# Layer-norm statistics of two tokens in one bn_stats instruction

## The chip, the cores and the metric

The kernel runs on one core of a Trainium2 chip. The core has a matrix engine (TensorE, PE in the profile), a vector engine (VectorE, DVE), a scalar engine (ScalarE, ACT), a general engine (GpSimd, POOL) and a queue of DMA commands (SyncE, SP). Each engine works through a list of instructions of its own in a fixed order and waits where an instruction needs what another engine has not finished. The metric is the device time of one execution in microseconds. The profile is one execution taken by the hardware profiler.

## The reference

The input is 32 images of 56 x 56 tokens with 96 channels each. Everything is float32 but for the feed-forward part, which rounds to small float formats.

```python
# layer 0: per token layer norm, matmul, 3 x 3 convolution
mu = jnp.mean(x, axis=-1, keepdims=True)
var = jnp.mean(jnp.square(x - mu), axis=-1, keepdims=True)
h = (x - mu) * jax.lax.rsqrt(var + LN_EPS) * ln_w + ln_b
x1, z = jnp.split(jnp.einsum('bhwc,cd->bhwd', h, w_in) + b_in, 2, axis=-1)
x = x + jax.nn.silu(conv3x3(x1) + conv_b)
# layer 1: attention by a Fourier transform over the 3136 tokens of an image
t = to_tokens(x)
t = t + bn2(w2 @ real(ifft(relu_mix(fft(relu(bn1(w1 @ ln(t)))))))) 
t = t + ffn(ln(t))           # 96 -> 384 -> 96, products of rounded values
```

So each token passes three layer norms. Each needs the mean and the variance of its 96 channels.

## The kernel before

**Layout.** An image lies in SBUF as 112 partitions x 28 tokens x 96 channels, so the channels of a token are next to each other in one partition. It is loaded in four chunks (LN_CHUNKS) of 8, 8, 8 and 4 tokens per partition. Most work goes by groups g of four tokens per partition, seven of them (NG) in an image.

**Three norms.** `stats(t, kind, b, i)` is called once for each kind, image and chunk. Kind "a" is the norm ahead of the convolution (tile xl, called in `take_in`), kind "b" the norm ahead of the Fourier part (tile t, in `conv_part`, as soon as the two groups of a chunk have been added), kind "c" the norm ahead of the feed-forward part (tile t again, in `back`). The tile t has 97 columns per token. The last column is for kind b, where L144 writes the square root of the variance into it.

**What stats does before.** One `bn_stats` for each token (L130) reads 96 channels and writes six numbers: a count, a mean and a sum of squared deviations of the channels in even places, and the same three of the channels in odd places. Five small instructions, each on all tokens of the chunk (8 or 4 columns), join the halves: the difference d of the two means (L135), the sum of the two squared sums with epsilon (L136), the mean for kind c alone (L139), and the variance with the term of d (L140 and L141). GpSimd raises the variance to the power of -1/2 (L142). For kinds a and b no mean is wanted, because the centring is folded into the weights that follow. `norm` runs on GpSimd: L153 subtracts the mean (kind c), L154 multiplies by the factor of L142.

**What runs beside it.** Four images are in flight. The outer loop over k has two parts in every turn. In the first, the spectrum part, TensorE does the second half of the Fourier transform (px at L252, pg at L279, pe at L284) and VectorE the mixing between them, five instructions each time (L266 to L271). In the second part, for each g, `forth` starts the transform of the next image (ph at L224, pa at L229), `back` ends that of the present one (py at L304; L305 adds py to t and frees its PSUM buffer, of which ph and px take the same two in turn) and calls stats c, and `ffn` runs the feed-forward part with a lag of four groups. There TensorE computes pf (L314), ScalarE rounds it to h1 (L316), VectorE adds the bias and clips (h2, L318) and rounds (hq, L319), TensorE multiplies again (po, L326), ScalarE and VectorE round and add (L330, L332), and GpSimd adds the result to t (L333). A list of pieces of later images, `filler`, is spread over both parts: the convolution (cv at L201), its adding to the image (L210), stats b, and stats a with the norm of an image further ahead.

**Order.** The kernel's text gives the instructions, the tile framework's scheduler gives each engine its order and the waits. The statistics tile, d and var come from the pool `stp` with three buffers for each tag, mean and factor from `sums` with eight.

Of the kernel before, what the change touches and what calls it, by code (L numbers as in the profile page):

```python
# [38 lines left out]
F32 = mybir.dt.float32  # L39
# [3 lines left out]
ALU = mybir.AluOpType  # L43
AX = mybir.AxisListType

C = 96
HW = 56
N = HW * HW
N1, N2 = 112, 28
# [12 lines left out]
EPS = 1e-5  # L62
# [17 lines left out]
def hybrid_kernel(ctx: ExitStack, tc: tile.TileContext, x, par, w_in, conv_w, w1, w2, fw1, fb1, fw2, fb2, fa, fb, ib, ia, on, out):  # L80
    nc = tc.nc
# [36 lines left out]
    sums = ctx.enter_context(tc.tile_pool(name="sums", bufs=8))  # L118
    stp = ctx.enter_context(tc.tile_pool(name="stp", bufs=3))
# [3 lines left out]
    def stats(t, kind, b, i):  # L123


        n = t.shape[1]
        name = f"{kind}_{b}_{i}"
        st = stp.tile([N1, n, 2, 3], F32, tag="st6", name=f"st6_{name}")
        for j in range(n):
            nc.vector.bn_stats(st[:, j].rearrange("p h s -> p (h s)"), t[:, j, :C])  # L130
        d = stp.tile([N1, n], F32, tag="d", name=f"d_{name}")
        var = stp.tile([N1, n], F32, tag="var", name=f"var_{name}")
        mu = None
        rs = sums.tile([N1, n], F32, tag=f"rs{kind}", name=f"rs_{name}")
        nc.vector.tensor_tensor(d, st[:, :, 0, 1], st[:, :, 1, 1], ALU.subtract)  # L135
        nc.vector.scalar_tensor_tensor(var, st[:, :, 0, 2], C * EPS, st[:, :, 1, 2], ALU.add, ALU.add)  # L136
        if kind == "c":
            mu = sums.tile([N1, n], F32, tag="mu", name=f"mu_{name}")
            nc.vector.scalar_tensor_tensor(mu, d, 0.5, st[:, :, 1, 1], ALU.mult, ALU.add)  # L139
        nc.vector.scalar_tensor_tensor(d, d, 0.25, d, ALU.mult, ALU.mult)  # L140
        nc.vector.scalar_tensor_tensor(var, var, 1.0 / C, d, ALU.mult, ALU.add)  # L141
        nc.gpsimd.tensor_tensor(rs, var, mhalf[:, :n], ALU.pow)  # L142
        if kind == "b":
            nc.vector.tensor_tensor(t[:, :, C], var, rs, ALU.mult)  # L144
        return mu, rs

    def norm(t, mu_rs, kind, b, i):

# [215 lines left out]
    def take_in(im, i):  # L364

        if i + 1 < len(LN_CHUNKS):
            fetch(im, i + 1)
        xl = im.xl.pop(i)
        im.xa += norm(xl, stats(xl, "a", im.b, i), "a", im.b, i)
# [8 lines left out]
    def conv_part(im, g):  # L378

        if g % 2 == 0 and g < NG:  # L380
            im.load(g // 2)
        if g < NG:
            im.s[g] = conv(im.strips.pop(g), im.b, g)
        if g >= 1:
            conv_add(im.s.pop(g - 1), im.group(g - 1, im.x), im.group(g - 1)[:, :, :C], im.b, g - 1)
            for i in ended(g - 1):
                im.rs[i] = stats(im.t[i], "b", im.b, i)[1]
# [18 lines left out]
    def back(im, g):  # L406

        transform_out(im.y.pop(g), im.group(g)[:, :, :C], im.b, g)
        fetch_y(im, g + 3)
        for i in ended(g):  # L410
            im.xc += norm(im.t[i], stats(im.t[i], "c", im.b, i), "c", im.b, i)
# [71 lines left out]
    with tc.tile_pool(name="setup", bufs=1) as sp, tc.tile_pool(  # L483
        name="setup_ps", bufs=2, space=bass.MemoryType.PSUM
# [247 lines left out]
```

## Time and profile before

| what | value |
|---|---|
| time, median of three runs | 4002.35 us (3998.4 to 4002.89) |
| span of the profiled execution | 3996.6 us |
| TensorE busy | 3660.6 us, 92% |
| VectorE busy | 2669.3 us, 67% |
| ScalarE busy | 2196.9 us, 55% |
| GpSimd busy | 1283.2 us, 32% |
| bn_stats, three kinds | 2,688 instructions, 509.1 us |

The busy time of an engine counts overlapping instructions once, so the sum over groups is larger than the busy time. In a line of a group, the first number behind the bar is the busy time in us, then the mean duration of one in ns; behind the second bar stands how long the engine was idle just before the instructions of the group, and who ended it. In a line of the timeline, start and duration in us come first, and a number in brackets is the idle time ahead of it with what ended it. A line of waits names who waited for whom, the total in us, how many times, and the longest.

### The profile page before, as it was taken

The page shows a single profiled execution, that of the slowest core. Times are in us where ns is not written, and L with a number is a line of the kernel's source. Part 1 is how long each engine was busy: PE and PEld are TensorE (multiplying, and loading weights), DVE is VectorE, ACT ScalarE, POOL GpSimd, SP SyncE. Part 2 cuts the span into 40 slices and gives each one's busy share as a digit, 9 for nine tenths or more (in the row PEclk, how much of TensorE's full clock was granted, in tenths as well). Part 3 has the DMA queues.
Part 4 walks back from the last instruction along what each step waited for, and adds up shares of the span by engine and source line. Part 5 has one row for each costly group of instructions (what it writes and reads, how often), then busy time and mean ns, then how long its engine had stood idle before and what let it go on. Part 6 is the DMA issues. An engine that isn't in the chain of part 4 may idle for free. (4 is left out here: it accounts for less than half of the span.)

```text
span 3996.6 us, 70615 instructions
## 1 busy us (share of the span) xinstructions
PE 3660.6 (92%) x22229; PEld 2482.5 (62%) x22229; DVE 2669.3 (67%) x9014; ACT 2196.9 (55%) x5154; POOL 1283.2 (32%) x1004
## 2 busy tenths in 40 slices
PE   5899999999999999999999999999999999999986
PEld 3566666566666566665566665666665666665665
DVE  3366677676677676677676676766676766676666
ACT  1355555555555555555555555555555555555564
POOL 2133223333233333233332233332243332243322
PEclk9999999999999999999999999999999999999996
DMA  5554455554555554545554445545545555555531
GB/s 137 141 151 133 135 140 139 143 150 137 138 138 140 145 149 137 137 128 149 142 144 130 134 136 140 156 136 139 138 137 141 152 138 136 140 137 143 143 87 52
DMA packets 582492, 546.30 MB, mean 137 GB/s; under 512 B 172584, under 2 KB 535304, under 8 KB 581896
## 3 DMA queue, kind: packets, MB, share of 16 engines
q1 hardware_dynamic: 578402, 539.17, 49.5%
q8 instruction: 180, 2.95, 0.3%
q10 hardware_dynamic: 3720, 2.63, 0.3%
q14 instruction: 190, 1.56, 0.1%
HBM read 346.93 MB, written 194.25 MB: 135 GB/s over the span
## 5 line engine op out<-in xcount | busy, mean ns | idle before, releaser
L201 PE MATMUL cv<-k,wp 128*96 128x448 f32 (+1 forms) x3136 | 1368.8, 550 | 21.6 <-ACT s L203 12.6
L201 PEld LDWEIGHTS cv<-k,wp 128*96 128x96 f32 (+1 forms) x3136 | 462.5, 165 | 385.1 <-issue 334.0
L316 ACT CAST h<-pf 128x448 f16<-128x448 f32 x672 | 358.7, 534 | 433.7 <-PE pf L314 415.3
L305 DVE TENSOR_TENSOR t<-py,t 112x384 f32<-112x384 f32 x224 | 124.5, 556 | 628.4 <-PE py L304 628.4
L153 POOL TENSOR_TENSOR xn_c<-t,mu_c 112x768 f32<-112x768 f32 (+1 forms) x128 | 169.0, 1321 | 1028.1 <-DVE var_a L136 826.4
L252 PE MATMUL px<-fb_sb,at 112*96 112x112 f32 (+1 forms) x3584 | 431.2, 263 | 24.8 <-DVE sv L268 18.9
L252 PEld LDWEIGHTS px<-fb_sb,at 112*96 112x96 f32 x3584 | 383.6, 165 | 78.9 <-DVE sv L268 30.3
L279 PE MATMUL pg<-w2a,gt 96*112 96x96 f32 (+1 forms) x3584 | 416.8, 264 | 12.9 <-DVE gt L271 10.8
L227 ACT ACTIVATE h<-ph,rs_b 112x192 f32<-112x192 f32 x896 | 325.2, 419 | 186.1 <-PE ph L224 175.1
L326 PEld LDWEIGHTS <-hq 128*112 128x112 fp8e5 x2688 | 207.7, 134 | 331.0 <-DVE hq L319 281.8
L224 PE MATMUL ph<-w1a,n2t 97*112 97x192 f32 x1792 | 365.1, 332 | 42.4 <-DVE t L305 41.7
L279 PEld LDWEIGHTS pg<-w2a,gt 96*112 96x112 f32 (+1 forms) x3584 | 383.1, 179 | 27.4 <-PE st L209 12.8
L318 DVE TENSOR_SCALAR h<-h,b1q 128x448 f16<-128x448 f16 x672 | 350.6, 522 | 62.7 <-ACT h L316 59.2
L203 ACT ACTIVATE s<-cv,par_sb 96x448 f32<-96x448 f32 x224 | 141.5, 632 | 456.5 <-PE cv L201 456.5
L142 POOL TENSOR_TENSOR rs_a<-var_a,mhalf 112x8 f32<-112x8 f32 (+1 forms) x128 | 199.4, 1558 | 590.0 <-DVE var_a L141 554.8
L142 POOL TENSOR_TENSOR rs_b<-var_b,mhalf 112x8 f32<-112x8 f32 (+1 forms) x128 | 192.4, 1503 | 587.7 <-DVE var_b L141 413.5
L326 PE MATMUL po<-w2q,hq 128*112 128x96 fp8e5 x2688 | 251.1, 220 | 141.7 <-DVE hq L319 131.6
L229 PE MATMUL pa<-h,fa_sb 112*112 112x384 f32 x896 | 369.4, 508 | 6.0 <-ACT h L227 1.4
L333 POOL TENSOR_TENSOR o<-t,y 112x384 f32<-112x384 f32 x224 | 201.2, 898 | 447.4 <-DVE y L332 261.2
L224 PEld LDWEIGHTS ph<-w1a,n2t 97*112 97x112 f32 x1792 | 281.3, 177 | 94.3 <-DVE t L305 61.3
L319 DVE CAST hq<-h 128x448 fp8e5<-128x448 f16 x672 | 315.6, 470 | 16.1
L266 DVE SCALAR_TENSOR_TENSOR sv<-px,par_sb,av 96x224 f32<-96x224 f32 (+1 forms) x448 | 197.8, 442 | 174.1 <-ACT av L264 172.8
(106 smaller groups left out, 6387.7 us busy)
## 6 DMA issues: line engine op xcount, KB each, us to landing
k<-img SPq DMA_DIRECT2D x2464, 58.0 KB
da<-u SPq DMA_DIRECT2D x224, 336.0 KB
at<-da SPq DMA_DIRECT2D x224, 336.0 KB
img<-stage SPq DMA_DIRECT2D x224, 174.0 KB
de<-es SPq DMA_DIRECT2D x224, 168.0 KB
y<-de SPq DMA_DIRECT2D x224, 168.0 KB
out<-o SPq DMA_DIRECT2D x224, 168.0 KB
xl<-in_x SPq DMA_DIRECT2D x96, 336.0 KB
```

What stands on the lines that cost most here:

```text
L142: nc.gpsimd.tensor_tensor(rs, var, mhalf[:, :n], ALU.pow)
L201: nc.tensor.matmul(ps, wp[: seen.shape[0], k, :], seen, start=(k == 0), stop=(k == 6))
L224: nc.tensor.matmul(ph[:, j, :], n2t[:, 2 * j2 + j, :], w1a, start=True, stop=True)
L227: nc.scalar.activation(h[:, j], ph[:, j], AF.Relu, scale=rs[:, 2 * j2 + j : 2 * j2 + j + 1])
L229: nc.tensor.matmul(pa, fa_sb, h, start=True, stop=True)
L252: nc.tensor.matmul(px[:, j], ats[g][:, j, i * C : (i + 1) * C], fb_sb[:, first(p) : first(p + 1)], start=True, stop=True)
L279: nc.tensor.matmul(pg[:, j, :], lhs, w2a[:, i, :], start=(i == 0), stop=(i == 1))
L316: nc.scalar.copy(h1, pf)
L318: nc.vector.tensor_scalar(h2, h1, b1q[:, k : k + 1], 0.0, ALU.add, ALU.max)
L319: nc.vector.tensor_copy(hq[:, k, :], h2, saturate=False)
L326: nc.tensor.matmul(po[:, j, :], hq[:, k, j * N1 : (j + 1) * N1], w2q[:, k, :], start=(k == 0), stop=(k == 2))
L333: nc.gpsimd.tensor_tensor(o, tg, y2, ALU.add)
```

## The change

One `bn_stats` now takes two tokens. It reads them channel by channel in turn: channel 0 of the first, channel 0 of the second, channel 1 of the first, and so on. The even places are then the first token and the odd places the second, so the six numbers are the statistics of two whole tokens and nothing has to be joined. What is left is one instruction per chunk: the sum of squared deviations divided by 96, plus epsilon. The mean for kind c is read where bn_stats wrote it, with a step of three. The statistics tile has a tag for each kind; d and mu are no longer there. It is for fewer instructions on VectorE.

```diff
-        st = stp.tile([N1, n, 2, 3], F32, tag="st6", name=f"st6_{name}")
-        for j in range(n):
-            nc.vector.bn_stats(st[:, j].rearrange("p h s -> p (h s)"), t[:, j, :C])
-        d = stp.tile([N1, n], F32, tag="d", name=f"d_{name}")
+        st = stp.tile([N1, n, 3], F32, tag=f"st{kind}", name=f"st_{name}")
+        for j in range(0, n, 2):
+            nc.vector.bn_stats(
+                st[:, j : j + 2].rearrange("p j s -> p (j s)"), t[:, j : j + 2, :C].rearrange("p j c -> p c j")
+            )
         var = stp.tile([N1, n], F32, tag="var", name=f"var_{name}")
-        mu = None
+        nc.vector.tensor_scalar(var, st[:, :, 2], 1.0 / C, EPS, ALU.mult, ALU.add)
         rs = sums.tile([N1, n], F32, tag=f"rs{kind}", name=f"rs_{name}")
-        nc.vector.tensor_tensor(d, st[:, :, 0, 1], st[:, :, 1, 1], ALU.subtract)
-        nc.vector.scalar_tensor_tensor(var, st[:, :, 0, 2], C * EPS, st[:, :, 1, 2], ALU.add, ALU.add)
-        if kind == "c":
-            mu = sums.tile([N1, n], F32, tag="mu", name=f"mu_{name}")
-            nc.vector.scalar_tensor_tensor(mu, d, 0.5, st[:, :, 1, 1], ALU.mult, ALU.add)
-        nc.vector.scalar_tensor_tensor(d, d, 0.25, d, ALU.mult, ALU.mult)
-        nc.vector.scalar_tensor_tensor(var, var, 1.0 / C, d, ALU.mult, ALU.add)
         nc.gpsimd.tensor_tensor(rs, var, mhalf[:, :n], ALU.pow)
         if kind == "b":
             nc.vector.tensor_tensor(t[:, :, C], var, rs, ALU.mult)
-        return mu, rs
+        return (st[:, :, 1] if kind == "c" else None), rs
```

The lines of the kernel after the change stand five lower from L142 on (L142 becomes L137).

## The prediction

> **What bounds the kernel now.** I read the page first (busy shares, then the slices), then the waits of TensorE in the steady stretch, then the groups of the lines that the change touches, and last the timeline of one image.
>
> ```profile
> PE 3660.6 (92%) x22229; PEld 2482.5 (62%) x22229; DVE 2669.3 (67%) x9014; ACT 2196.9 (55%) x5154; POOL 1283.2 (32%) x1004
> PE   5899999999999999999999999999999999999986
> DVE  3366677676677676677676676766676766676666
> ```
>
> TensorE (PE) is busy in nine tenths of every slice but the first two and the last two; VectorE (DVE), where the whole change lies, is at two thirds. So VectorE's own busy time is not the time of the kernel. What counts is how often TensorE stands waiting for it. Between 250 and 3780 us TensorE is busy for 3296.59 of 3530 us: it idles 233 us there, and some 103 us more in start and end. The waits of TensorE in that stretch, longest first:
>
> ```profile
> PE po L326 <- DVE hq L319: 119.0, 123, 2.1
> PE ph L224 <- DVE t L305: 41.7, 29, 2.6
> PE px L252 <- DVE sv L268: 18.1, 57, 0.4
> PE pf L314 <- DVE n3t L310: 12.6, 30, 0.4
> PE cv L201 <- ACT s L203: 9.7, 29, 0.3
> PE pg L279 <- DVE gt L271: 8.2, 29, 0.5
> ```
>
> Columns: total us, times, longest. About 200 us of the 233 have VectorE as releaser, none of them a line of the statistics. The statistics matter only as what stands ahead of L319 and L305 in VectorE's queue. The groups that go:
>
> ```profile
> L130 DVE BATCH_NORM_STATS2 st_a<-xl 112x6 f32<-112x96 f32 x896 | 172.4, 245 | 80.3 <-DMA xl<-in_x 80.3
> L141 DVE SCALAR_TENSOR_TENSOR var_c<-var_c,d_c 112x8 f32<-112x8 f32 (+1 forms) x128 | 79.3, 620 | 2.3
> L140 DVE SCALAR_TENSOR_TENSOR d_c<-d_c 112x8 f32<-112x8 f32 (+1 forms) x128 | 52.8, 412 | 0.2
> L136 DVE SCALAR_TENSOR_TENSOR var_c<-st_c 112x8 f32<-112x8 f32 (+1 forms) x128 | 20.5, 160 | 0.0
> ```
>
> One operation of eight columns takes 160 ns, yet L141 averages 620. The timeline of one stall shows why:
>
> ```profile
> 2061.16 0.56 DVE L305 TENSOR_TENSOR t<-py,t 112x384 f32<-112x384 f32 x1 [1.75 <-PE py L304]
> 2061.76 0.74 DVE L130 BATCH_NORM_STATS2 st_c<-t 112x6 f32<-112x96 f32 x4
> 2062.53 0.83 DVE L135 TENSOR_TENSOR d_c<-st_c 112x8 f32<-112x8 f32 x1
> ...
> 2063.89 1.27 DVE L141 SCALAR_TENSOR_TENSOR var_c<-var_c,d_c 112x8 f32<-112x8 f32 x1
> ...
> 2067.03 1.41 DVE L141 SCALAR_TENSOR_TENSOR var_a<-var_a,d_a 112x8 f32<-112x8 f32 x1
> 2068.36 0.54 DVE L305 TENSOR_TENSOR t<-py,t 112x384 f32<-112x384 f32 x1
> ```
>
> ```profile
> 2063.64 1.49 POOL L153 TENSOR_TENSOR xn_c<-t,mu_c 112x768 f32<-112x768 f32 x1 [0.32 <-DVE mu_c L139]
> 2066.95 1.47 POOL L154 TENSOR_TENSOR xn_c<-xn_c,rs_c 112x768 f32<-112x768 f32 x1
> ```
>
> ```profile
> 2068.96 0.90 PE L224 MATMUL ph<-w1a,n2t 97*112 97x192 f32 x4 [2.40 <-DVE t L305]
> ```
>
> The reader sees a queue, not a dependence. Between two L305 lie 12 bn_stats, the small operations and two L141 that end with GpSimd's L153 and L154. L305 comes 7.20 us after its predecessor, and TensorE loses 2.40 us.
>
> [...] 1.27 and 1.41 us for an operation that else takes 0.16, ending with GpSimd's 1.49 and 1.47. [...] L305 and L130 keep their durations here. [...] the timeline has eight bn_stats within 1.36 us, (1.36-0.245)/7 = 159 ns from start to start. [...] The new bn_stats alternates between two tokens. No instruction of the trace reads SBUF so; the nearest, ScalarE's L203, reads PSUM alternately from two halves and takes 632 ns for 448 elements, where the plain copy L215 takes 537, so 1.2 times.
>
> **The change part by part.**
> 1. bn_stats: 2,688 of 96 elements become 1,344 of 192. A pair occupies VectorE for 2 x 159 = 318 ns now. [...] I take the full rate: [...] the L203 comparison points the same way.
> 2. Small operations: L135, L136, L140, L141 go in 384 chunks and L139 in 128, 1,664 in all; 384 tensor_scalar come. The timeline has them 85 ns apart, so -1,280 x 0.085 = -109 us.
> 3. Waiting for GpSimd inside them: over 0.163 us each, L141 of c and a, L140 of c and L135 of c hold 58, 42, 32 and 19 us, 151 us in all. I do not expect all to go: [...] the mean now needs no work, so L153 is released by the last bn_stats itself and can start just ahead of the tensor_scalar. I count half, -75 us; the ends are 0 and -151.
> 4. L153 reads its mean from the statistics tile with a step of three. It has its own three buffers for c, freed when L153 ends, a whole chunk before they are wanted. GpSimd runs the same 1,004 instructions and has two thirds of its time free: nothing.
> 5. Order. A scheduler places the work; in the changed program the TensorE order of a steady image is the same but for a few transposes and matmuls moved by one or two places. On VectorE, in the stretch of the stall above, 8 bn_stats of pairs and two tensor_scalar stand between the L305 of group 3 and that of group 4, and near the end of an image the add of h2 stands ahead of the column write (L144) that waits some 1.8 us for GpSimd's rs, not behind it.
>
> Sum for VectorE: -78 - 109 - 75 = -262 us of 2669. Most of that lies beside a busy TensorE. What reaches the end: (a) the stall on L305. Of its 7.20 us, L305 and L210 keep 1.1; [...] two small ones 0.2, and one or two waits for GpSimd 1.2 to 2.4 make 4.6 to 5.8. That is 1.4 to 2.6 us earlier, against a mean stall of 41.7/29 = 1.44 us; I take off 30 of 41.7 us. (b) L319: 119/29 = 4.1 us per image. The last piece, 1.99 us in the image that I read, is caused by L144 standing ahead of h2, and half of it should go; another, 1.26 us, is an L318 that met L154 of the next image, which now comes 1.5 us earlier and may miss it. The others are GpSimd meetings that the change does not touch. I take 1 us per image, 30 us. (c) Start and end: the chain of the last image holds L141 of c (1.24 us), and the first image passes four such; 3 us. Sum -63 us: 4002 - 63 = 3939, say 3940 us.
>
> **The rivals.** There are three.
> The alternating read is slow [...]. [...] In (a) [...] about 10 us of gain; in (b) the last piece only, 12 us. 4002 - 25 = 3977 us.
>
> TensorE hides nearly everything: the stalls on L319 stay, since GpSimd's L153, L154 and L333 meet L318 and L319 whatever the statistics cost, and L305 gains a little. For: the 119 us are mostly such meetings. Against: 41.7 us stand behind the statistics alone. 3998 us.
>
> Slower: [...] With 1 us per image lost, 4002 + 32 = 4034 us. A moved meeting with GpSimd ahead of L319 would end in the same place.
>
> **How the numbers follow.** Full rate and gains as summed: 0.5. Slow read with a small gain: 0.24. Nothing to be seen: 0.1. Slower: 0.16. The first two are faster by more than 0.2% (8 us), but a part of the second falls short of it, so faster 0.72, same 0.1, slower 0.18. The lower end of the range is the forecast with all of the 151 us gone, the whole L305 stall (42), 60 us of L319 and 10 of start and end: 4002 - 112 = 3890. The upper end takes in the second and third case and the nearer half of the fourth: 4018.
>
> **What would show it.** Right: about 345 ns for the new bn_stats [...], VectorE near 2,400 us, the wait of ph for t under 15 us, that of po for hq under 105. Step 1 is wrong if the new bn_stats takes 470 ns or more; step 3 if the new tensor_scalar averages 160 ns (all gone) or 600 (none gone, in fewer instructions). The forecast is wrong in kind if VectorE falls by 250 us and TensorE's wait for hq stays at 119: then GpSimd, not the statistics, holds that path.

## The result and the profile after

The changed kernel takes 3858.18 us (3856.06 to 3861.2), the kernel before 4000.38 us in the same runs: a ratio of 0.9645 with a 95% interval of 0.9628 to 0.9662, so 142 us less. The forecast was 63 us less, and 3858 lies below the lower end of its range, 3890.

From the page of the changed kernel, the busy times and then TensorE's busy share in 40 slices of the span:

```profile
PE 3615.4 (94%) x22229; PEld 2468.4 (64%) x22229; DVE 2405.9 (62%) x6390; ACT 2190.8 (57%) x5154; POOL 1294.3 (34%) x1004
...
PE   6899999999999999999999999999999999999987
```

VectorE lost 263 us, as forecast (262). What the forecast did not have is in the first number: TensorE has the same 22,229 matmuls, and yet its busy time fell by 45 us, from 3660.6. The rest of the gain is idle time: span less busy was 336.0 us and is 238.9, so 97 us. 45 + 97 = 142.

The waits of TensorE in the steady stretch, 250 to 3640 us, after:

```profile
PE po L321 <- DVE hq L314: 77.1, 80, 1.7
PE px L247 <- PE tp_n L157: 27.8, 48, 0.9
PE pf L309 <- DVE n3t L305: 16.4, 12, 1.4
```

The wait of ph for t (41.7 us before) is gone, and so are those of px for sv (18.1) and of pg for gt (8.2); po for hq fell from 119.0 to 77.1. A wait of px for TensorE's own transposes has come up (27.8, from 0.9); what lies behind it was not traced further. In sum the steady stretch idles 145 us (3390 less 3244.88 busy), where it was 233.

The groups of the changed lines:

```profile
L131 DVE BATCH_NORM_STATS2 st_c<-t 112x6 f32<-112x192 f32 x448 | 142.8, 354 | 5.1
L131 DVE BATCH_NORM_STATS2 st_a<-xl 112x6 f32<-112x192 f32 x448 | 142.5, 351 | 314.3 <-DMA xl<-in_x 314.3
L135 DVE TENSOR_SCALAR var_c<-st_c 112x8 f32<-112x8 f32 (+1 forms) x128 | 74.7, 584 | 1.2
L135 DVE TENSOR_SCALAR var_a<-st_a 112x8 f32<-112x8 f32 (+1 forms) x128 | 58.7, 459 | 0.7
L139 DVE TENSOR_TENSOR t<-var_b,rs_b 112x8 f32<-112x8 f32 (+1 forms) x128 | 41.5, 324 | 174.4 <-POOL rs_b L137 174.4
L135 DVE TENSOR_SCALAR var_b<-st_b 112x8 f32<-112x8 f32 (+1 forms) x128 | 22.2, 173 | 5.6
```

A bn_stats of a pair takes 351 to 354 ns, where the forecast was 345, and 470 or more if step 1 was wrong. The L135 of kind b takes 173 ns in the mean; those of c and a take 584 and 459, so some still wait for GpSimd, as one of 1.40 us in the timeline below does. The last but one line has the largest idle time among these that another engine ends: VectorE stands still for 174.4 us ahead of the column write, of which the forecast had little to say. (The 314.3 us ahead of kind a are waits for the load of an image.)

The timeline of the same place in an image as that of the stall that the prediction showed, VectorE and then GpSimd:

```profile
2107.14 0.56 DVE L300 TENSOR_TENSOR t<-py,t 112x384 f32<-112x384 f32 x1 [1.86 <-PE py L299]
2107.74 0.63 DVE L131 BATCH_NORM_STATS2 st_c<-t 112x6 f32<-112x192 f32 x2
2108.28 0.35 DVE L131 BATCH_NORM_STATS2 st_a<-xl 112x6 f32<-112x192 f32 x1
2108.55 1.40 DVE L135 TENSOR_SCALAR var_c<-st_c 112x8 f32<-112x8 f32 x1
...
2111.39 0.15 DVE L135 TENSOR_SCALAR var_a<-st_a 112x8 f32<-112x8 f32 x1
2111.46 0.36 DVE L131 BATCH_NORM_STATS2 st_b<-t 112x6 f32<-112x192 f32 x1
2111.73 0.54 DVE L300 TENSOR_TENSOR t<-py,t 112x384 f32<-112x384 f32 x1
```

```profile
2108.44 1.48 POOL L148 TENSOR_TENSOR xn_c<-t,st_c 112x768 f32<-112x768 f32 x1 [0.42 <-DVE st_c L131]
```

From one L300 (L305 before) to the next it is now 4.59 us instead of 7.20. One of the two waits for GpSimd is left, on var_c, which ends with L148 (at 2109.95 and 2109.92 us) as step 3 of the prediction expected; var_a goes through in 0.15 us. TensorE no longer waits for t here.

### The profile page after: what moved, and what is told of

The parts are those of the page before. It is cut to its first block, busy times and chain, and to the rows that moved or that the text cites. A ratio compares the mean times of both kernels' runs of the same rounds, so it can differ in the third digit from the quotient of the medians.

```text
span 3854.3 us, 68115 instructions
## 1 busy us (share of the span) xinstructions
PE 3615.4 (94%) x22229; PEld 2468.4 (64%) x22229; DVE 2405.9 (62%) x6390; ACT 2190.8 (57%) x5154; POOL 1294.3 (34%) x1004
## 5 line engine op out<-in xcount | busy, mean ns | idle before, releaser
L148 POOL TENSOR_TENSOR xn_c<-t,st_c 112x768 f32<-112x768 f32 (+1 forms) x128 | 169.7, 1326 | 996.8 <-DVE st_c L131 922.9
L137 POOL TENSOR_TENSOR rs_b<-var_b,mhalf 112x8 f32<-112x8 f32 (+1 forms) x128 | 194.0, 1516 | 608.6 <-DVE var_b L135 425.6
L300 DVE TENSOR_TENSOR t<-py,t 112x384 f32<-112x384 f32 x224 | 124.3, 555 | 437.5 <-PE py L299 437.3
L137 POOL TENSOR_TENSOR rs_a<-var_a,mhalf 112x8 f32<-112x8 f32 (+1 forms) x128 | 199.2, 1556 | 552.8 <-DVE var_a L135 530.4
L313 DVE TENSOR_SCALAR h<-h,b1q 128x448 f16<-128x448 f16 x672 | 310.0, 462 | 99.4 <-ACT h L311 93.9
L131 DVE BATCH_NORM_STATS2 st_a<-xl 112x6 f32<-112x192 f32 x448 | 142.5, 351 | 314.3 <-DMA xl<-in_x 314.3
L321 PE MATMUL po<-w2q,hq 128*112 128x96 fp8e5 x2688 | 241.3, 220 | 86.1 <-DVE hq L314 85.9
L314 DVE CAST hq<-h 128x448 fp8e5<-128x448 f16 x672 | 310.8, 463 | 15.4
## 6 DMA issues: line engine op xcount, KB each, us to landing
da<-u SPq DMA_DIRECT2D x224, 336.0 KB
at<-da SPq DMA_DIRECT2D x224, 336.0 KB
xl<-in_x SPq DMA_DIRECT2D x96, 336.0 KB
```

The source lines that it names most:

```text
L313: nc.vector.tensor_scalar(h2, h1, b1q[:, k : k + 1], 0.0, ALU.add, ALU.max)
L314: nc.vector.tensor_copy(hq[:, k, :], h2, saturate=False)
L321: nc.tensor.matmul(po[:, j, :], hq[:, k, j * N1 : (j + 1) * N1], w2q[:, k, :], start=(k == 0), stop=(k == 2))
```

## The experiments

### Which part of the change brings the gain

**Joins gone.** The bn_stats of before, one for each token, but none of the joining: only the statistics of the even channels are used, those of the odd ones are left out.

```diff
-            nc.vector.bn_stats(
-                st[:, j : j + 2].rearrange("p j s -> p (j s)"), t[:, j : j + 2, :C].rearrange("p j c -> p c j")
-            )
+            nc.vector.bn_stats(st[:, j].rearrange("p h s -> p (h s)"), t[:, j, :C])
-        nc.vector.tensor_scalar(var, st[:, :, 2], 1.0 / C, EPS, ALU.mult, ALU.add)
+        nc.vector.tensor_scalar(var, st[:, :, 0, 2], 2.0 / C, EPS, ALU.mult, ALU.add)
```

> One bn_stats per token as before, but the five joining instructions are gone and one tensor_scalar takes their place, so the statistics are those of the even channels alone (the odd half is left out). VectorE loses 1,280 short instructions and no bn_stats time. Theory Q (the length of VectorE's queue ahead of L305 and L319 is what counts): the joins are some 185 of the 263 us that the whole change took from VectorE, so about two thirds of the 142 us: 3,900 to 3,915 us. Theory G (what counts is that fewer instructions meet GpSimd's long reads): nearly everything, 3,855 to 3,875 us. Theory B (the shorter bn_stats are what counts): 3,970 to 4,000 us.

Measured: 3875.29 us, ratio 0.969 (0.9676 to 0.9705), 124 us less than before. VectorE 2447.4 us, TensorE busy 3612.1 us.

**Pairs, joined.** New bn_stats of pairs, but with as many small instructions as before; they add a difference that is zero, so that only their time counts. The tiles for d and for the mean come back with them, and the statistics of all kinds share one tag again.

```diff
+        nc.vector.tensor_tensor(d, st[:, :, 1], st[:, :, 1], ALU.subtract)
+        nc.vector.scalar_tensor_tensor(var, st[:, :, 2], C * EPS, st[:, :, 2], ALU.add, ALU.max)
+        if kind == "c":
+            nc.vector.scalar_tensor_tensor(mu, d, 0.5, st[:, :, 1], ALU.mult, ALU.add)
+        nc.vector.scalar_tensor_tensor(d, d, 0.25, d, ALU.mult, ALU.mult)
+        nc.vector.scalar_tensor_tensor(var, var, 1.0 / C, d, ALU.mult, ALU.add)
```

> bn_stats on two tokens as after the change, with the five joining instructions kept in their old dependence (d is the mean minus itself, so the result is the same). Theory Q: a third of the gain, 3,945 to 3,965 us, and the two parts add up to about 142 us. Theory G: 3,980 to 4,000 us. Theory B: 3,860 to 3,890 us. If both parts alone give most of the gain, or neither does, it is a threshold (the stall at L305 vanishes once the queue is short enough).

Measured: 3923.41 us, 0.9809 (0.9792 to 0.9825), 76 us less; VectorE 2560.0 us. Each part brings something alone, the joins more. Neither of the first two theories fits both runs: the first time lies at the upper end of what G gave, the second 22 us below what Q gave. Together the parts bring 142 and not 124 + 76 = 200, and the two take the same waits away: the wait of ph for t (41.7 us before) is 0 in the first and 5.9 us in the second, that of po for hq (119.0) 77.7 and 75.6 us, where the whole change leaves 0 and 77.1.

**Two tokens in a row.** The pair is read token after token, so that the two halves are no longer single tokens.

```diff
-                st[:, j : j + 2].rearrange("p j s -> p (j s)"), t[:, j : j + 2, :C].rearrange("p j c -> p c j")
+                st[:, j : j + 2].rearrange("p j s -> p (j s)"), t[:, j : j + 2, :C]
```

> After the change, but bn_stats reads its two tokens one after the other and not in turn, so each half mixes two tokens (other statistics, same amount of work). If alternating costs nothing per element: bn_stats stays at 350 ns and the time within 0.3% of 3,858 us. If alternating costs even 0.1 ns per element: bn_stats at 333 ns or less.

```profile
L131 DVE BATCH_NORM_STATS2 st_a<-xl 112x6 f32<-112x192 f32 x448 | 140.9, 348 | 319.6 <-DMA xl<-in_x 319.6
L131 DVE BATCH_NORM_STATS2 st_c<-t 112x6 f32<-112x192 f32 x448 | 140.6, 349 | 5.1
```

348 and 349 ns against 351 and 354, and for kind b 346 against 352: the alternating read costs 3 to 6 ns in 192 elements. A single execution took 3865.78 us, about that of the changed kernel. The rival of the slow read (470 ns or more) is refuted by a direct measurement.

**One kind alone.** The new statistics for kind a, b or c, the old ones for the other two.

```diff
+        if kind in ("a",):
+            ...
+            return (st[:, :, 1] if kind == "c" else None), rs
+        st = stp.tile([N1, n, 2, 3], F32, tag="st6", name=f"st6_{name}")
+        ...
```

> The change for kind a alone; b and c as before. In the kernel before, the wait for hq of group 4 (35.7 us in all) follows an h2 that met L154 of kind a, and it is gone in every changed version. If the shorter way to var of kind a is the cause: group 4 falls under 5 us, the stall of ph for t (41.7 us) by a third or more since 6 of the 12 bn_stats ahead of L305 and L141 of a go, and the time to 3,930 to 3,955 us. If it is VectorE's queue in general: half of the whole gain or less in group 4.

> The change for kind c alone; a and b as before. Kind c has L305, its bn_stats, five joining instructions and two meetings with GpSimd in one queue; if that queue makes the stall of ph for t: 41.7 us fall under 15 us, group 4 of hq stays near 36 us, and the time is 3,940 to 3,965 us. If group 4 falls too, it hangs on the whole queue and not on kind a.

> The new statistics for kind b alone; a and c keep the old ones. Kind a alone gave -59 us, c alone -44, all three -142. If the kinds simply add up, b gives -39 us: 3,962 us. Theory of the hold: b's chain is shorter by some 1.0 us per chunk (4 x 0.06 of bn_stats, four small operations of 0.085, what they wait), but the column write still stands about 1.8 us for GpSimd in VectorE's queue, so the wait of po for hq stays over 100 us and the time is 3,950 to 3,985. If the statistics' own time in VectorE's queue is what counts, b gives a third of the whole, -47 us, and the wait of po for hq falls to near 100 too.

| new for kind | us | ratio, interval | less by | VectorE us | TensorE busy us | po for hq us |
|---|---|---|---|---|---|---|
| a | 3942.01 | 0.9854 (0.9839 to 0.9869) | 59 | 2530.5 | 3668.6 | 86.9 |
| c | 3957.24 | 0.9893 (0.9879 to 0.9908) | 44 | 2507.5 | 3676.0 | 125.6 |
| b | 3922.59 | 0.9802 (0.9785 to 0.9818) | 78 | 2574.0 | 3634.3 | 94.4 |

The gain is not in proportion to VectorE's saving: c saves it the most (162 us) and brings the least, b the least (95 us) and brings the most, twice what was expected of it. Kind b is the one whose chain ends at the column write. In a and c TensorE's busy time even rose over the 3660.6 of before. Behind this, and behind the order of the three, stands the clock: stretches in which TensorE runs at half clock, counted as in the part on why the prediction was wrong, cost 55 us before, and 72, 79 and 35 us with a, c and b. The mean granted clock of the profiled executions was 0.983 before and 0.979, 0.977 and 0.988 with a, c and b. With this cost as before, an estimate from these numbers, a would have brought 76 us, c 68 and b 58. In a and c 20 of the 21 and all 25 half-clock stretches of the steady part follow the wait of po for hq of the last group of an image, which is 2.0 us there as it was before; with b it is 1.65 us, and no half-clock stretch follows it.

The wait of po for hq of group 4, 35.7 us before, is 0.3 us with a, 26.0 with c and 11.4 with b: it hangs on kind a above all, as expected. The wait of ph for t is gone in a and in c alone, so this stall needed only part of the room; with b 21.4 us of it are left.

### What holds VectorE's queue

After all this VectorE still stood idle for 174.4 us ahead of the column write, the product of var and rs into the 97th column of t for kind b. It waits for GpSimd's power. Before the change, the group of the column write and one place on VectorE's timeline:

```profile
L144 DVE TENSOR_TENSOR t<-var_b,rs_b 112x8 f32<-112x8 f32 (+1 forms) x128 | 41.5, 324 | 192.6 <-POOL rs_b L142 192.6
```

```profile
2084.05 0.17 DVE L141 SCALAR_TENSOR_TENSOR var_b<-var_b,d_b 112x8 f32<-112x8 f32 x1
2086.05 0.17 DVE L144 TENSOR_TENSOR t<-var_b,rs_b 112x8 f32<-112x8 f32 x1 [1.83 <-POOL rs_b L142]
2086.13 0.55 DVE L305 TENSOR_TENSOR t<-py,t 112x384 f32<-112x384 f32 x1
```

For 1.83 us the engine does nothing, and L305, whose input py has been ready since 2085.16, stands behind it. After the change, in the feed-forward stretch, on VectorE and on TensorE:

```profile
2034.19 0.34 DVE L313 TENSOR_SCALAR h<-h,b1q 128x448 f16<-128x448 f16 x1
2036.07 0.85 DVE L139 TENSOR_TENSOR t<-var_b,rs_b 112x8 f32<-112x8 f32 x1 [1.54 <-POOL rs_b L137]
2036.83 0.38 DVE L314 CAST hq<-h 128x448 fp8e5<-128x448 f16 x1
```

```profile
2037.27 0.25 PE L321 MATMUL po<-w2q,hq 128*112 128x96 fp8e5 x1 [1.67 <-DVE hq L314]
```

The column write is now behind the add of h2 (L313), but still ahead of the cast to hq, and TensorE loses 1.67 us.

**The column write on GpSimd**, directly behind the power there: once in the changed kernel, once in the kernel before and with nothing else changed.

```diff
-            nc.vector.tensor_tensor(t[:, :, C], var, rs, ALU.mult)
+            nc.gpsimd.tensor_tensor(t[:, :, C], var, rs, ALU.mult)
```

> After the change, with the write of the column of kind b (var times rs, L139) on GpSimd right behind the power, so that VectorE no longer stands still for GpSimd (174 us of waits at that line). Theory Q: part of the 77 us that TensorE waits for hq is behind this line, about 1 us per image: 3,815 to 3,840 us. If those waits are only L313 and L314 meeting GpSimd's reads: within 10 us of 3,858.

> The kernel before with one edit: the column write of kind b (L144) on GpSimd. In the kernel before, TensorE waits 57.8 us for hq of the last group of an image (group 6), 29 times, and after the change still 48.2 us, because L144 (then L139) stands in VectorE's queue until GpSimd's power is done. If that is the cause: group 6 falls to about 10 us here as well, and the time by 60 to 90 us, to 3,910 to 3,940 us, without any change to the statistics. If group 6 waits for meetings with GpSimd's reads: no more than 15 us.

| | column on VectorE | column on GpSimd |
|---|---|---|
| statistics of before | 4001 | 3796.5 (3793.94 to 3803.27), ratio 0.9494 (0.948 to 0.9508) |
| new statistics | 3858.2 | 3779.35 (3777.68 to 3782.51), ratio 0.945 (0.9436 to 0.9464) |

The edit of one word in the kernel before brings 205 us, more than the whole change and far more than the 60 to 90 us that were expected of it. The mechanism was as expected: the wait of po for hq of the last group, 57.8 us before, is gone. The size was not: between the profiled executions TensorE's idle time falls by 136 us over the whole span and its busy time by 59. With this edit in place the change is worth 17 us and not 142. The waits of TensorE in the kernel before with the column on GpSimd, 250 to 3600 us:

```profile
PE po L326 <- DVE hq L319: 43.4, 89, 1.3
PE ph L224 <- DVE t L305: 29.9, 29, 2.6
```

and in the changed kernel with it, 250 to 3560 us, which is the best version found:

```profile
PE po L321 <- DVE hq L314: 30.3, 74, 0.7
PE pf L309 <- DVE n3t L305: 20.7, 15, 1.4
```

VectorE is busy for 2640.9 us in the first, 28 less than before, and 2405.9 us in the changed kernel: the one with 235 us more work on VectorE is 62 us faster. From the first to the second TensorE's idle time falls by 39 us more, but its busy time rises by 15; this rise was not traced. The column costs GpSimd 31.2 us (244 ns each).

**The column write later.** In the kernel before, it stays on VectorE but is issued in the next step of the convolution. The scheduler then puts operations of the spectrum ahead of it; in the feed-forward stretch its place stays the same.

```diff
-            nc.vector.tensor_tensor(t[:, :, C], var, rs, ALU.mult)
+            later_col.append(lambda: nc.vector.tensor_tensor(t[:, :, C], var, rs, ALU.mult))
...
+            column()
             conv_add(im.s.pop(g - 1), im.group(g - 1, im.x), im.group(g - 1)[:, :, :C], im.b, g - 1)
```

> The kernel before, with the column write issued later in VectorE's queue: in the spectrum stretch five operations of the spectrum now stand ahead of it, so that GpSimd's power is over by then; in the feed-forward stretch (the chunks that end with groups 1 and 3 of the convolution) it stays directly behind var_b, as before. VectorE's work is the same. Moving it to GpSimd took 205 us off. Theory: what counts is VectorE standing still, and the part on TensorE's path is the one in the feed-forward stretch: then the waits of px for sv and pg for gt (26 us) fall by half or more, po for hq stays at 110 to 120, the idle time before the column write falls from 193 to about 100 us, and the time is 3,960 to 3,985. Rival: the standing still in the spectrum stretch is worth as much as that in the other: 3,890 to 3,920. Third: it was VectorE's 41 us of work on the column: no change, 4,000.

Measured: 3918.47 us, 0.9793 (0.9778 to 0.9807), 82 us less, with VectorE at 2642.1 us. VectorE stands still ahead of the column write for 122.7 us in place of 192.6:

```profile
L150 DVE TENSOR_TENSOR t<-var_b,rs_b 112x8 f32<-112x8 f32 (+1 forms) x128 | 40.1, 313 | 122.7 <-POOL rs_b L148 122.7
```

The whole fall is in the two column writes of an image that lie in the spectrum stretch (76 to 6 us in sum); the other two keep 116 us. The waits of px for sv and pg for gt are all but gone (0.4 us left), ph for t fell from 41.7 to 11.2, po for hq from 119.0 to 100.0. The work on the column is the same, so these 82 us are no work saved: they come of the order in VectorE's queue, and with it of the standing still. How the rest of the 205 us divides between the standing still in the feed-forward stretch and the 41.5 us of work that left VectorE was not separated. The part in the spectrum stretch is worth far more than the 26 us of waits that name it: the waits of ph for t and of po for hq, in the other stretch, fell by 50 us too. Half-clock stretches cost 65 us here, 10 more than before, so they do not explain the gain. The time is the one that the rival gave, not the theory.

**Variance and column on GpSimd**, in the changed kernel.

```diff
-        nc.vector.tensor_scalar(var, st[:, :, 2], 1.0 / C, EPS, ALU.mult, ALU.add)
+        nc.gpsimd.tensor_scalar(var, st[:, :, 2], 1.0 / C, EPS, ALU.mult, ALU.add)
```

> After the change, with both what is left of the joins (var, L135) and the column write on GpSimd, so that VectorE does bn_stats alone. L135 costs VectorE 144 us after the change, 584 ns each for kind c, of which 400 ns are a wait for GpSimd's L148. Theory Q: 10 to 25 us less than with the column alone (3,779): 3,755 to 3,770. If GpSimd's own chain ahead of tp_n gets longer by more than that saves: 3,785 to 3,810.

Measured: 3806.97 us, 0.9522 (0.9506 to 0.9538): 28 us slower than with the column alone, although VectorE has 83 us less to do (2302.2) and its last waits for GpSimd in the statistics are gone. The wait of po for hq went up from 30.3 to 74.9 us. GpSimd's chain is now var (205 to 219 ns) and the power (about 1.52 us). The growth of the wait is in the first and third of the seven groups of an image (10.5 to 40.3 and 0 to 18.6 us), and L313 and L314, which make hq, last 509 and 513 ns in the mean where they lasted 441 and 483. Which instructions of GpSimd they met was not separated.

## Why the prediction was wrong

**Step 1 (bn_stats) held.** 351 to 354 ns for 345 forecast, 106 to 111 ns more than a bn_stats of one token (241 to 246 ns). By groups the three kinds take 429.4 us in place of 509.1, so 80 us less where the sum took 78. What the alternating read would cost was the author's estimate in the forecast and in its rivals alike: no trace from before the change has a bn_stats that reads so. The run with the tokens in a row (346 to 349 ns) shows that it costs 3 to 6 ns here.

**Steps 2 and 3 (small operations, waits) held nearly.** The joins of a and c waited 151 us over their bare duration; L135 still waits 54 us for c (74.7 - 128 x 0.163) and 38 us for a, so 59 us went where 75 were taken. The waits that are left for c come by the route that step 3 named: L148 starts ahead of var_c. VectorE's sum came out right, 263 us, with two terms that the forecast did not have and that nearly cancel: the h2 add and the cast to hq cost it 42 us less, other operations 35 us more.

**Step 4 (L153 reading the statistics) held** as far as durations show: L148 takes 1326 ns, L153 took 1321; GpSimd is busy for 1294.3 us against 1283.2.

**The sum "what reaches the end" failed**, in the term that it does not have. It priced a stall of TensorE by the idle time that the profile shows and took the 3660.6 us of busy time as fixed work, so that it put at nothing what became 45 us. The terms that it had were sized too small as well, but their 97 us are less than the 112 us at the end of its range; it is the missing term that takes the time past it. Measured term by term:

| term | forecast us | measured us |
|---|---|---|
| (a) ph for t on L305 | -30 | -42 |
| (b) po for hq on L319 | -30 | -42 |
| other waits of the steady stretch | 0 | -4 (sv -18, gt -8, own transposes +27, n3t +4, small ones -9) |
| (c) start and end | -3 | -9 |
| TensorE's busy time | 0 | -45 |

In (a) the mean of 1.44 us mixed two stalls: 22 of the 29 are 1.12 us long and seven 2.4 to 2.6 us, the one shown among these. All are gone.

Two things in the traces make up the 45 us. First, by an estimate from these traces, a stall is longer than the profile shows. A transpose of 112 columns (L162) is recorded for 258 ns in the median, but in the median the next one starts 96 ns after it; when none follows, the first 258 - 96 ns, 0.16 us, of the stall are counted as busy. The steady stretch had 517 gaps between matmuls and has 305. Second, behind a part of the long stalls the granted clock was 0.50. The stretches around the stall that the prediction showed, before the change; columns are length, busy us of PE, PEld, DVE, ACT and POOL with their instructions, granted clock, DMA share, GB/s:

```profile
2063.43:2066.84 3.41, 3.07 (x13) 1.74 (x12) 3.38 (x16) 1.81 (x6) 3.10 (x2) 1.00 0.44 115
2066.84:2070.26 3.42, 1.30 (x9) 1.21 (x10) 3.39 (x11) 0.84 (x3) 3.16 (x4) 1.00 0.77 209
2070.26:2073.67 3.41, 3.41 (x8) 1.73 (x7) 2.07 (x6) 2.22 (x6) 1.45 (x1) 0.50 0.49 126
2073.67:2077.08 3.41, 3.41 (x25) 2.03 (x23) 3.38 (x14) 0.91 (x2) 0.81 (x1) 1.00 0.72 173
```

TensorE idles 2.1 us of the second stretch, and in the third, where it is busy all through, the clock is 0.50. It does 8 matmuls there. By an estimate from the clock, half of the 3.41 us, 1.7 us, is lost and counted as busy. The steady stretch before the change has 11 such stretches at half clock, the one after has none. How much each is worth can be counted. Take the time from the start of each matmul to the start of the next, and subtract the median that the same pair of matmuls has in all twelve traces at full clock and without a gap. What is over, less the recorded gap, is time counted as busy in which TensorE did not work at its pace:

| time over the median, whole span | before us | after us | change us |
|---|---|---|---|
| ahead of a recorded gap, at full clock | 92 | 59 | -33 |
| in half-clock stretches | 55 | 33 | -22 |
| neither | 99 | 109 | +9 |

The sum is the 45 us, up to rounding. Of the 22, 19 are the 11 stretches of the steady part, 1.7 us each; the rest is in start and end. The rise of 9 us was not traced. No run put in a stall of a chosen length; that half-clock stretches came of stalls rests on the counts over twelve traces in the last part.

The number of half-clock stretches went with a small difference in one wait. Five of the 11 follow one of the seven long stalls of ph for t, six the wait of po for hq of the last group of an image. That wait was 2.0 us, 29 times, and is 1.66 us after the change, where none of the 29 is followed by a half-clock stretch. The prediction had no such step; that no half-clock stretch followed the shorter wait is luck.

**(b) had about the right size by the wrong route, which is luck.** By the group of four tokens that po works on, summed over the 29 images: the piece caused by the h2 add meeting L154 of the next image, of which the prediction said that it "may miss it", was 35.7 us and is 0.3. The last piece, behind the column write, of which half should go, was 57.8 us and is 48.2. A new piece, 12.9 us in the first group, takes some of the gain back. The prediction noted that the add of h2 gets ahead of L144; the cast that follows it does not.

**What the prediction did not ask** is what the change would be worth with the column write out of the way. It named L144 and its 1.8 us only as the cause of one stall. The two-by-two table shows it as the hold on VectorE's queue in all stretches: shorter statistics are worth 142 us behind it and 17 us without it. That they make up lost time behind it fits this, but no run shows it apart from the rest. The other rivals (TensorE hides nearly all, slower) are refuted by the time itself. In the chances, the part of the second case that falls short of 8 us was given to "slower" (0.16 became 0.18), where "same" is its place.

## What to carry to other kernels

When one engine bounds a kernel and another makes it wait now and then, price a stall by more than the idle time that is recorded: here each shows too short by the tail of the matmul before it (an estimate of up to 0.16 us), and some of the long ones were followed by a stretch at a granted clock of 0.5, which appears as busy time (1.7 us each). When two variants are compared, look at whether the clock made the difference. Before shortening work on an engine that isn't full, look in its groups for the largest idle time ahead of one small instruction: here one that waited for a round trip to another engine held what was queued behind it (1.83 us in the place shown), and moving it to the engine that it waited for was worth more (205 us) than 263 us less work (142 us).

## What the runs showed of the hardware

**Half clock came behind pieces with much idle time.** In the trace of before, each stretch at a granted clock of 0.5 begins a whole number of pieces of 3.413 us after the first one, and each in the steady stretch lasts one piece. The steady stretches of the twelve traces, from 250 us to 216 us before the end, were cut in pieces on this grid. All 68 pieces in which TensorE was recorded idle for 1.9 us or more were followed at once by a piece at a granted clock of 0.5. Of 162 pieces with 1.4 to 1.9 us idle 23 were, and of the 11,757 with less one, the second of two in a row at the beginning of a steady stretch. In the trace of before these are 8 of 8, 3 of 15 and none of 1,011; in that of the changed kernel no piece was idle for 1.9 us, and none of the 16 and none of the 976 with less was followed so. With kind c alone an image takes 119.7 us, which is close to 35 pieces (119.5 us), so that the stall falls at nearly the same place of a piece in one image after another: 20 of the 24 steps between its half-clock stretches are of 35 pieces, the other four of 70.

**The alternating read of bn_stats cost next to nothing**: 3 to 6 ns in 192 elements (351 to 354 ns against 346 to 349), so 0.02 to 0.03 ns per element, for two tokens 384 or 388 bytes apart.

**A tensor_scalar of eight columns also waited for GpSimd.** In the timeline above L135 of var_c takes 1.40 us where L148 runs beside it and ends with it, and L135 of var_a 0.15 us where GpSimd runs the power on eight columns.
